# Eight steps of lag in attention, tails without row-wide POOL work, and rows weighed as their gathers land

## The chip, the cores and the metric

The kernel runs on one core of a Trainium2 chip. The metric is the device time of one execution in microseconds (us); lower is better. Engines are called PE (matrix products, with PEld for its weight loads), DVE (vector), ACT (activations), POOL (GpSimd) and SP (the queue that issues most DMAs). Each engine runs its own instructions strictly in the order in which the program emitted them.

## The reference

Input: eight batches of 512 rows with 128 features, float32. Six residual sublayers follow each other:

```python
x = x + 0.5 * moe(layernorm(x))        # stage 0: 8 experts, each row goes to its best 2
x = x + attention(layernorm(x))        # stage 1: 16 heads of 8, causal, rotary positions
x = x + 0.5 * moe(layernorm(x))        # stage 2: the same experts again
x = x + 0.5 * fp6_linear(layernorm(x)) # stage 3
x = x + mixer(layernorm(x))            # stage 4
x = x + 0.5 * fp6_linear(layernorm(x)) # stage 5

def moe(x):        # gates: softmax over the two best scores; y = relu(x W1 + b1) W2 + b2
    return sum(gate[e] * expert[e](x) for e in best_two)

def fp6_linear(x): # blocks of 32: scale = max|x| / 7.5, values rounded to a 6-bit grid
    return dequantized(x) @ dequantized(weight).T + bias

def mixer(x):
    xn = rmsnorm(x) * w1
    h  = scan(h = a * h + sigmoid(g) * tanh(v)), a = 0.001 + 0.998 * sigmoid(d)   # g, v, d: products of xn
    x  = x + h
    xn = rmsnorm(x) * w2
    return x + (silu(xn Wg.T) * (xn Wu.T)) Wo.T
```

## The kernel before

All eight batches stay in SBUF as tiles `X[b]` of 128 partitions x 4 x 128: four groups of 128 rows. The program is one long Python function that emits instructions; the order on each engine is what the generators below yield to each other.

**The planner.** `Clock` (L66) logs every instruction that a generator emits between two yields, adds estimated durations (`took`) and keeps, for each engine, the time at which it would be free, and for each generator the time at which its next step is `ready`. `drive` (L141) follows one main generator and lets side generators step at given rates when they are ready; `finish` (L159) always steps the stream that is ready first. No time of the chip enters: the planner only fixes the order. A step that yields `"product"` must be due; another one may come 0.7 planned us early.

**MoE.** The batches of a MoE stage go in two groups (stage 2: batches 0 to 4, then 5 to 7). A router (`moe_front`, in stage 2 `moe_stream`, batch by batch) scores rows, finds the two best experts and scatters the normed rows with POOL's indirect DMAs into a table in DRAM sorted by expert. `moe_tiles` runs tiles of 256 rows: SP loads the expert's weights and the rows, PE turns and multiplies, ACT and DVE apply relu (`hs`), DVE copies (`xt`) and adds the last bias (`yo`), SP stores to `rows_out`. Stage 2 has 27 tiles for its first group and 19 for its second. `moe_combine` gathers each row's two results from `rows_out` with POOL's indirect DMAs into tiles `y` (six buffers) and weighs them into `X[b]` with two DVE operations for each 128 rows (`put`, which runs when more than three gathered tiles wait). `behind` holds a generator back until a condition is true: the gathers of a group start when all its tiles' stores are emitted (`filled`).

**Attention** runs in steps t; one unit is a batch and one of four head groups, three steps long, and two units make a pair. In step t `maxima` computes scores of unit (t + LAG) // 3 on PE (tiles `sa`) and DVE takes their row maxima (`seen`, into `nstat`); `shifted` turns a pair's maxima on PE (`tp_st`) and adds them into the queries (`qa`); `weights` computes the scores again with the maxima taken off (`sb`), ACT takes the exponentials (`pm`), POOL zeroes what is masked; `values` multiplies by V (`av`). `PIECES_A` and `PIECES_C` list which row blocks a step computes: its scores of four strips of PE run side by side. `pre(b)` (projections, rotary) and `post(b)` are side streams inside the loop. Scores and other products share eight PSUM banks. The stage-2 router and tiles run beside attention as side streams.

**Tails.** After a batch's stage-2 rows are weighed, `tail(b)` does `fp6`, `mix`, `fp6` and the output DMA; up to four tails are in flight (`flight`), and `Slots` limit how many are in a given part. `fp6` (L1277): moments on DVE, a power of -0.5 on POOL, normed rows `um` on ACT, then `quantized` (L1227): block maxima and reciprocals on DVE, the product with the reciprocal on POOL, the rounding by four DVE operations, the product with the scale on POOL; then turned on PE, copied by ACT, multiplied by the weight, and added by DVE. POOL also adds half the bias to `X[b]`. `mix` (L1307) norms twice, one after the other (layer norm to `um_m`, then the rms norm to `row_m`, each with its own power on POOL), runs three gate products, tanh on ACT, the scan on DVE, a second norm from DVE's moments, six products with silu, and the last product; POOL adds `um_m` to `X[b]`.

Most instructions carry the line of the recording helper, L185, so profiles of this kernel are read by tile names.

Of the kernel before, what the change touches and what calls it, by code (L numbers as in the profile page):

```python
# [46 lines left out]
LANDING = 5  # L47
AHEAD = 4
# [17 lines left out]
class Clock:  # L66
# [4 lines left out]
    def __init__(self, nc):  # L71
        self.free = dict.fromkeys(("tensor", "vector", "scalar", "gpsimd"), 0.0)
        self.log = []
        self.ready = {}
        self.slack = {}
        self.flowing = set()
        for name in self.free:
            setattr(self, name, _Logged(getattr(nc, name), name, self.log))
# [19 lines left out]
    def account(self, ready, chained=True):  # L98
# [3 lines left out]
        for engine, op, out, args in self.log:  # L102
# [9 lines left out]
            if op == "indirect_dma_start":  # L112
                end += 0.5
# [3 lines left out]
    def step(self, gen, now):  # L117

        self.log.clear()
        hint = next(gen, gen)  # L120
# [38 lines left out]
    def finish(self, *streams, until=None):  # L159
# [3 lines left out]
        while live and not (until and until()):  # L163
            g = min(live, key=lambda g: max(self.ready.get(g, 0.0), now))
            now = max(now, min(self.ready.get(g, 0.0), max(self.free.values())))
# [69 lines left out]
def kernel(  # L235
# [112 lines left out]
    half_bq = cpool.tile([P, P], F32, tag="half_bq", name="half_bq")  # L348
# [5 lines left out]
    nc.sync.dma_start(out=half_bq, in_=bq.partition_broadcast(P))  # L354
# [6 lines left out]
    def clear_for_attention():  # L361
# [11 lines left out]
        ck.gpsimd.tensor_scalar_mul(half_bq, half_bq, 0.5)  # L373
# [121 lines left out]

    def sent(s, g):
# [8 lines left out]
    def need(s, b):  # L505

        while (s, b) not in done:
            if next(backlog[0], backlog) is backlog:
                backlog.pop(0)
            ck.idle(ck.free["tensor"] + 0.5)  # L510

# [155 lines left out]
    def moe_stream(s, g):  # L667
# [81 lines left out]
        for n, b in enumerate(bs):  # L749
# [16 lines left out]
            ms = []  # L766
            for k in range(2):
# [3 lines left out]
                ck.vector.tensor_tensor(is_max, l, m.to_broadcast([P, NT, NE]), ALU.is_equal)  # L771
                ck.vector.tensor_tensor(is_max, is_max, rank, ALU.mult)
# [10 lines left out]
            ck.vector.tensor_tensor(both, oh[:, 0, sl, :], oh[:, 1, sl, :], ALU.add)  # L783
            ck.vector.tensor_tensor(ex[:, sl].unsqueeze(2), ms[1], ms[0], ALU.subtract)
            yield "product"
# [14 lines left out]
            ck.vector.tensor_tensor(place, place, in_tile, ALU.add)  # L800
            ck.vector.tensor_tensor(
# [6 lines left out]
            )  # L808
            ck.vector.tensor_reduce(at_f[:, :, sl], q, AX.X, ALU.add)
# [22 lines left out]
    def moe_tiles(s):  # L832
# [55 lines left out]
        def second(i, h):  # L888
# [21 lines left out]
            ))  # L910
            del T[i]
# [33 lines left out]
    def moe_combine(s, g):  # L945
# [7 lines left out]
        def put():  # L953
            f, y, t, b = waiting.pop(0)
            f(y, t)
            if t == NT - 1:
                done.add((s, b))

        for n, b in enumerate(GROUPS[s][g]):
# [9 lines left out]
            for t in range(NT):  # L969
# [11 lines left out]
                waiting.append((weighted, y, t, b))  # L981
                if len(waiting) > 3:
                    put()
        while waiting:
            yield
            put()


    def attention(bs, s):
# [6 lines left out]
        PIECES_A = [[(1, 0)], [(3, 0)], [(2, 0), (0, 3 * P)]]  # L996
        PIECES_C = [[(0, 0)], [(1, 0), (3, 3 * P)], [(2, 0)]]
        LAG = 7
# [228 lines left out]
    def quantized(src, g, name, slots=None, also=None):  # L1227
# [19 lines left out]
        ck.gpsimd.tensor_tensor(y, src, along(rs), ALU.mult)  # L1247
        if also:
            also()
        yield  # L1250
# [6 lines left out]
        ck.vector.tensor_scalar(m, m, 1.5, 2.0**20, ALU.max, ALU.mult)  # L1257

        ck.vector.scalar_tensor_tensor(t, y, -(2.0**-21), m, ALU.add, ALU.add)
        ck.vector.tensor_tensor(t, t, m, ALU.subtract)  # L1260
        yield
        ck.gpsimd.tensor_tensor(y, t, along(sc), ALU.mult)
# [14 lines left out]
    def fp6(b, s):  # L1277
# [6 lines left out]
        def plus_bias():  # L1284
            ck.gpsimd.tensor_tensor(
                X[b], X[b], half_bq.unsqueeze(1).to_broadcast([P, NT, P]), ALU.add
            )

        xd = yield from quantized(
            u.rearrange("p t (g k) -> p (t g) k", k=FB), S // FB, name, rounding, plus_bias  # L1290
        )
        yield from turning.take()
        xt = yield from by_feature(xd.rearrange("p (t g) k -> p t (g k)", t=NT), f"xd_{name}")
        rounding.give()
        yp = bank(f"yp_{name}")
        for t in range(NT):
            ck.tensor.matmul(yp[:, ts(t, P)], xt[:, ts(t, P)], wd_t, start=True, stop=True)
# [9 lines left out]
    def mix(b):  # L1307
        mv = moments(X[b], f"m_{b}")
        rs = yield from power(mv[:, :, 1], 1e-5, f"m_{b}")

        r2 = small.tile([P, NT], F32, tag="r2", name=f"r2_{b}")
# [209 lines left out]
```

## Time and profile before

| what | value |
|---|---|
| median of 4 runs | 1194.34 us (1193.94 to 1198.65) |
| the profiled execution | 1199.84 us, its span 1198.1 us |
| mean granted PE clock | 0.901 of full |
| attention's first scores to its last (`sa` to `sb`) | 276.6 to 820.6 us |
| last attention output added | 840.1 us |
| second group's expert tiles (`xp`) | 880.3 to 967.9 us |
| gathers of stage 2, group 0 and group 1 | 876.6 to 981.5, 998.0 to 1065.4 us |
| output stores issued | 1017.2, 1053.5, 1093.6, 1101.1, 1135.6, 1169.0, 1183.2, 1194.8 us |

How to read the profile lines: times count from the first instruction. A group or timeline line has engine, operation, `out<-in` by the program's tile names, partitions x elements, then count, duration (busy us and mean ns in groups) and the idle time of the engine just before, with what ended it. Two operations of one engine may overlap by some tenths of a microsecond. A line of waits is: engine and tile that waited, for whom, us in total, times, longest. A line of a stretch is: stretch, length, busy us (and instructions) of PE, PEld, DVE, ACT, POOL, granted PE clock, DMA share, GB/s. The slices of the page cut the span in 40; each digit is the busy share in tenths.

### The profile page before, as it was taken

The numbers are of one execution on the slowest core, as the hardware profiler recorded it, in microseconds if no ns is written. First come the engines' busy times: TensorE is split into PE (matmuls) and PEld (weight loads), VectorE is DVE, ScalarE is ACT, GpSimd is POOL, SyncE is SP. The second block draws the span as 40 slices with busy tenths as digits, with TensorE's granted clock in tenths as the row PEclk, the third lists the DMA queues.
The fourth block names the chain that finished last, engine by engine and source line by source line (L and its number), as shares of the span: only waits on it lengthen the run. The fifth ranks groups of instructions, "written<-read, shape, count | busy, mean of one in ns | idle before, by whom it ended". The sixth has DMA issues, their size and how long they took to land.

```text
span 1198.1 us, 20686 instructions
## 1 busy us (share of the span) xinstructions
PE 970.6 (81%) x6705; PEld 663.0 (55%) x6705; DVE 706.3 (59%) x2636; ACT 482.8 (40%) x1063; POOL 543.6 (45%) x694
## 2 busy tenths in 40 slices
PE   3261599899999899999999899999969895576583
PEld 2250599787754444444445366667859773344352
DVE  6040132455578877777768765632526867987774
ACT  1210133233255545454555444454314553444351
POOL 3637302511166676536364514132244757765432
PEclk9996799899999998889899999999979997797586
DMA  9542377687386000000000244234467510000000
GB/s 292 178 143 79 124 224 229 205 272 230 114 243 176 21 30 19 19 1 19 1 19 6 81 137 133 87 122 145 127 195 238 167 38 30 24 27 19 9 1 26
DMA packets 122363, 127.33 MB, mean 106 GB/s; under 512 B 9616, under 2 KB 103696, under 8 KB 122256
## 3 DMA queue, kind: packets, MB, share of 16 engines
q1 hardware_dynamic: 114064, 109.22, 29.6%
q0 software_dynamic: 8192, 16.79, 4.4%
q8 instruction: 53, 0.87, 0.3%
q14 instruction: 54, 0.44, 0.1%
HBM read 79.58 MB, written 46.40 MB: 105 GB/s over the span
## 4 chain that ended last, share of the span: by engine, by line
PE 61%; DVE 18%; another core or an unknown queue 6%; issue 5%; POOL 5%; ACT 3%; DMA 1%; SPq 1%; POOLq 0%; DVEq 0%; ACTq 0%
PE yp L185 14%; PE hp L185 13%; PE sa L185 10%; PE av L185 6%; PE sb L185 4%; DVE q L185 3%; DVE seen L185 2%; DVE x L185 2%; POOL y L185 2%; DVE st L185 2%; PE xp L185 2%; PE gt L185 1%; PE lp L185 1%; PE up L185 1%
## 5 line engine op out<-in xcount | busy, mean ns | idle before, releaser
L185 DVE CUSTOM_DVE_ANT_0 seen<-sa,future_s 128x128 f32<-128x128 f32 (+3 forms) x512 | 224.8, 487 | 91.2 <-PE sb L185 69.0
L185 ACT ACTIVATE pm<-sb 128x512 f32<-128x512 f32 (+1 forms) x384 | 182.8, 525 | 191.0 <-PE sb L185 165.2
L185 ACT ACTIVATE hs<-hp,wx 128x256 f32<-128x256 f32 x276 | 120.0, 471 | 313.5 <-PE hp L185 226.7
L185 PE MATMUL yp<-wx,hs 128*128 128x128 f32 x1472 | 204.0, 282 | 46.6 <-ACT hs L185 26.6
L185 PE MATMUL sb<-qa,ka 32*128 32x512 f32 (+3 forms) x1024 | 229.5, 490 | 8.2 <-DVE nstat L185 6.8
L185 PEld LDWEIGHTS yp<-wx,hs 128*128 128x128 f32 x1472 | 189.1, 195 | 63.4 <-ACT hs L185 27.7
L185 PE MATMUL hp<-xt,wx 128*128 128x256 f32 x736 | 200.8, 398 | 8.0 <-DVE g L185 5.3
L185 PE MATMUL sa<-ka,qz 32*128 32x256 f32 (+3 forms) x1024 | 205.5, 485 | 1.6 <-issue 1.6
L185 POOL TENSOR_SCALAR_AFFINE_SELECT pm<-pm 128x256 f32<-128x256 f32 x256 | 101.1, 409 | 215.1 <-ACT pm L185 206.8
L185 POOL DMA_INDIRECT y<-rows_out,at x128 | 134.4, 1050 | 135.9 <-DMA rows_out<-yo 85.7
L185 DVE TENSOR_SCALAR hs<-hp,wx 128x256 f32<-128x256 f32 x92 | 44.5, 483 | 204.2 <-ACT hs L185 178.3
L185 PEld LDWEIGHTS hp<-xt,wx 128*128 128x128 f32 x736 | 133.7, 201 | 31.2 <-issue 10.6
L185 PEld LDWEIGHTS sa<-ka,qz 32*128 32x128 f32 x1024 | 98.1, 192 | 65.9 <-issue 21.4
L185 PEld LDWEIGHTS sb<-qa,ka 32*128 32x128 f32 x1024 | 107.9, 192 | 26.6 <-DVE nstat L185 12.9
L185 PE MATMUL av<-pm,vpad 128*32 128x512 f32 (+3 forms) x1024 | 94.3, 464 | 0.0
L185 POOL DMA_INDIRECT by_stretch<-um,sat x64 | 64.3, 1005 | 30.2 <-issue 14.4
L185 POOL TENSOR_TENSOR rs<-rs,mhalf 128x4 f32<-128x4 f32 (+1 forms) x36 | 39.9, 1109 | 81.6 <-DVE rs L185 77.3
L185 PEld LDWEIGHTS av<-pm,vpad 128*32 128x32 f32 x1024 | 23.7, 110 | 69.4 <-issue 43.2
L185 POOL DMA_INDIRECT rows_in<-a,at x40 | 38.9, 973 | 31.8 <-issue 31.2
L185 DVE TENSOR_TENSOR yo<-yp,wx 128x256 f32<-128x256 f32 x92 | 38.4, 418 | 25.1 <-PE yp L185 10.2
L185 DVE SCALAR_TENSOR_TENSOR x<-y,g,x 128x128 f32<-128x128 f32 x128 | 51.8, 406 | 2.3
L185 PE MATMUL xp<-cst,xs 128*128 128x128 f32 x184 | 37.5, 290 | 16.5 <-DMA xs<-by_stretch 16.5
(219 smaller groups left out, 1316.4 us busy)
## 6 DMA issues: line engine op xcount, KB each, us to landing
wx<-in_wexp SPq DMA_DIRECT2D x92, 578.0 KB
rows_out<-yo SPq DMA_DIRECT2D x92, 128.0 KB
by_stretch<-zero SPq DMA_DIRECT2D x8, 1280.0 KB
rows_in<-zero SPq DMA_DIRECT2D x2, 3456.0 KB
by_stretch<-zero SPq DMA_DIRECT2D x8, 768.0 KB
xs<-rows_in SPq DMA_DIRECT2D x46, 128.0 KB
xs<-by_stretch SPq DMA_DIRECT2D x46, 128.0 KB
x<-in_x SPq DMA_DIRECT2D x8, 256.0 KB
```

What stands on the lines that cost most here:

```text
L185: return call(*args, **kw)
```

## The change

Five things change together.

1. Attention: `LAG` 7 becomes 8, and the first two entries of `PIECES_A` change places. The maxima run one step further ahead of the weights; the same widths lie beside each other as before. What hangs on the lag (`pre`, `masked`, `keyed`) moves one step with it.
2. `fp6`: the two row-wide products of `quantized` move from POOL to DVE. The bias goes into the product's PSUM bank as a matmul of a row of ones with the bias row (K = 1), ahead of the four weight products; POOL's addition and the halving of the bias are gone.
3. `mix`: both scalings of the first two norms come from one power of eight columns; the rms norm's rows `xn` are made first, the layer norm's `u` after the gates. The gate d's affine step moves from DVE to ACT. The second norm's mean square comes from four ACT squares with an accumulated sum instead of DVE's moments. `X[b] + u` is a matmul with the identity into the last product's bank instead of a POOL addition.
4. `moe_combine`: a gathered tile is weighed when the planner's clock is `FETCH` (3 us) past its gather, or when more than four wait; `landed` lets a group's gathers start 5 planned us after its last store instead of at once.
5. The planner: a gather's step is over when issued, other POOL operations cost 0.5 us more, `finish` may move its clock past all engines, and the stage-2 router yields more often (five more in a batch).

```diff
+FETCH = 3
@@ Clock.account
             if op == "indirect_dma_start":
+                end = at
+            elif engine == "gpsimd":
                 end += 0.5
@@ Clock.finish
-            now = max(now, min(self.ready.get(g, 0.0), max(self.free.values())))
+            now = max(now, self.ready.get(g, 0.0))
@@
+    def landed(s, g):
+        return filled(s, g) and ck.now >= groups[s, g]["since"] + LANDING
@@ moe_stream (one of the five places)
                 ck.vector.tensor_tensor(is_max, l, m.to_broadcast([P, NT, NE]), ALU.is_equal)
+                yield
                 ck.vector.tensor_tensor(is_max, is_max, rank, ALU.mult)
...
             ck.vector.tensor_tensor(ex[:, sl].unsqueeze(2), ms[1], ms[0], ALU.subtract)
-            yield "product"
+            yield
@@ moe_combine
+        def come():
+            return ck.now >= waiting[0][-1] + FETCH
...
-                waiting.append((weighted, y, t, b))
-                if len(waiting) > 3:
+                waiting.append((weighted, y, t, b, ck.free["gpsimd"]))
+                while len(waiting) > 4 or (waiting and come()):
                     put()
+                    yield
         while waiting:
-            yield
-            put()
+            if come():
+                put()
+            yield
@@ attention
-        PIECES_A = [[(1, 0)], [(3, 0)], [(2, 0), (0, 3 * P)]]
+        PIECES_A = [[(3, 0)], [(1, 0)], [(2, 0), (0, 3 * P)]]
...
-        LAG = 7
+        LAG = 8
@@ quantized
-        ck.gpsimd.tensor_tensor(y, src, along(rs), ALU.mult)
-        if also:
-            also()
-        yield
+        ck.vector.tensor_tensor(y, src, along(rs), ALU.mult)
...
         ck.vector.tensor_tensor(t, t, m, ALU.subtract)
-        yield
-        ck.gpsimd.tensor_tensor(y, t, along(sc), ALU.mult)
+        ck.vector.tensor_tensor(y, t, along(sc), ALU.mult)
@@ fp6
-        def plus_bias():
-            ck.gpsimd.tensor_tensor(
-                X[b], X[b], half_bq.unsqueeze(1).to_broadcast([P, NT, P]), ALU.add
-            )
...
+        ck.tensor.matmul(
+            yp.rearrange("p (t d) -> p t d", t=NT), ones[0:1, :],
+            bq_s[0:1].unsqueeze(1).to_broadcast([1, NT, P]), start=True, stop=False,
+        )
@@ mix
-        rs = yield from power(mv[:, :, 1], 1e-5, f"m_{b}")
-        r2 = small.tile([P, NT], F32, tag="r2", name=f"r2_{b}")
-        ck.vector.tensor_tensor(r2, rs, rs, ALU.mult)
-        ck.vector.tensor_tensor(r2, r2, mv[:, :, 1], ALU.mult)
-        u = yield from normed_act(X[b], mv, rs, f"m_{b}", tag="um")
-        rr = yield from power(r2, 1e-6, f"ma_{b}")
-        ck.vector.tensor_tensor(rr, rr, rs, ALU.mult)
-        xn = yield from normed_act(X[b], mv, rr, f"m_{b}", tag="row")
+        ck.vector.tensor_scalar(
+            rs2[:, 1], mv[:, :, 1], 1.0 + 1e-6, 1e-6 * 1e-5, ALU.mult, ALU.add
+        )
+        ck.vector.tensor_scalar_add(rs2[:, 0], mv[:, :, 1], 1e-5)
+        yield
+        ck.gpsimd.tensor_tensor(
+            rs2, rs2, mhalf[:, 0 : 2 * NT].rearrange("p (k t) -> p k t", k=2), ALU.pow
+        )
...
+        scaled(xn, 1, 0, NT)
...
-        ck.vector.tensor_scalar(d, d, 0.499, 0.5, ALU.mult, ALU.add)
+        ck.scalar.activation(d, d, AF.Copy, scale=0.499, bias=0.5)
+        scaled(u, 0, 0, NT)
...
-        mv = moments(u, f"f_{b}")
+            ck.scalar.activation(
+                xf[:, t, :], u[:, t, :], AF.Square, accum_out=r2[:, t : t + 1]
+            )
...
-        ck.gpsimd.tensor_tensor(X[b], X[b], u, ALU.add)
...
         yo = bank(f"yo_{b}")
+        ck.tensor.matmul(yo, ident, uf, start=True, stop=False)
@@
-    back = behind(moe_combine(2, 0), lambda: filled(2, 0) and sent(2, 1))
+    back = behind(moe_combine(2, 0), lambda: landed(2, 0) and sent(2, 1))
...
-    last = behind(moe_combine(2, 1), lambda: filled(2, 1))
+    last = behind(moe_combine(2, 1), lambda: landed(2, 1))
```

## The prediction

> **What bounds the kernel now.** I read the page first (busy shares and the slices), then the busy times by stretch, then the chain of waits and the waits of single engines in the stretches that the change touches, and last the timeline of the final fp6 pass.
>
> ```profile
> PE 970.6 (81%) x6705; PEld 663.0 (55%) x6705; DVE 706.3 (59%) x2636; ACT 482.8 (40%) x1063; POOL 543.6 (45%) x694
> ...
> PE   3261599899999899999999899999969895576583
> ...
> DVE  6040132455578877777768765632526867987774
> ...
> POOL 3637302511166676536364514132244757765432
> ```
> ```profile
> 275.00:845.00 570.00, 539.28 (x4339) 313.72 (x4340) 376.65 (x1569) 274.82 (x596) 255.77 (x412) 0.95 0.28 84
> 845.00:880.00 35.00, 26.17 (x171) 23.56 (x169) 15.89 (x65) 8.43 (x21) 10.61 (x11) 0.92 0.36 111
> 880.00:1000.00 120.00, 98.77 (x598) 84.57 (x598) 80.80 (x258) 50.41 (x113) 66.58 (x63) 0.90 0.49 151
> 1000.00:1125.00 125.00, 78.02 (x320) 50.42 (x320) 103.68 (x306) 55.24 (x124) 82.78 (x77) 0.73 0.07 21
> 1125.00:1198.00 73.00, 48.93 (x201) 31.50 (x200) 41.52 (x118) 28.60 (x61) 22.78 (x20) 0.76 0.04 15
> ```
> Each row gives the stretch, its length, then PE, PEld, DVE, ACT and POOL busy, the granted clock, DMA. Attention (275 to 845) is PE's: 539 of 570 us. From 880 to 1000 the last expert tiles run beside the first tails, PE still ahead with 99 of 120. From 1000 on it is tails alone: DVE has 104 of 125 us and POOL 83, PE 78 at a clock of 0.73. After 1125 no engine is near full; the last batches wait through their own chains. From 905, just before the first tail's start at 911, to the end DVE is busy 219.5 of 293 us.
>
> The chain of waits between 1000 and 1125, summed by engine from its pieces, is DVE 71 us, POOL 26, issue 16, PE 6, ACT 5: two engines hand rows to and fro. The final fp6 pass shows how:
>
> ```profile
> 1183.93 0.25 DVE L185 RECIPROCAL rs<-sc 128x16 f32<-128x16 f32 x1
> 1184.35 1.05 POOL L185 TENSOR_TENSOR q<-um,rs 128x512 f32<-128x512 f32 x1 [4.07 <-DVE rs L185]
> 1185.36 1.26 POOL L185 TENSOR_TENSOR x<-x,half_bq 128x512 f32<-128x512 f32 x1
> 1185.44 1.93 DVE L185 TENSOR_SCALAR q<-q 128x512 int32<-128x512 int32 x2 [1.25 <-POOL q L185]
> 1187.40 0.69 DVE L185 SCALAR_TENSOR_TENSOR q<-q,q 128x512 f32<-128x512 f32 x1
> 1188.13 0.69 DVE L185 TENSOR_TENSOR q<-q,q 128x512 f32<-128x512 f32 x1
> 1188.96 1.05 POOL L185 TENSOR_TENSOR q<-q,sc 128x512 f32<-128x512 f32 x1 [2.34 <-DVE q L185]
> ```
> PE's transposes start at 1190.06. Two things cost: POOL takes 1.05 us where DVE's like form takes 0.69, with a handover each way; and the two TENSOR_SCALARs take 1.93 beside POOL's bias add, where the pair takes 0.88 with POOL silent (1154.87). Taking each DVE form's undisturbed duration off its instructions from 905 to 1198, 30 us are excess, 29 of them overlapping POOL's row-wide operations (bias 12.4, x<-x,um_m 7.4, q 9.5) and 0.6 its gathers; 18 us of it lie between 1000 and 1125.
>
> Waits, as engine, whom it waited for, us, times, longest: of POOL (880 to 1070), DVE (1000 to 1125), PE (275 to 850).
> ```profile
> POOL y L185 <- DVE x L185: 9.6, 2, 7.7
> ...
> POOL y L185 <- DMA rows_out<-yo: 6.2, 1, 6.2
> ```
> ```profile
> DVE q L185 <- POOL q L185: 7.7, 2, 6.4
> ```
> ```profile
> PE tp_st L185 <- DVE nstat L185: 7.2, 5, 2.1
> PE sb L185 <- DVE nstat L185: 6.8, 10, 1.5
> ...
> PE pt L185 <- DVE k L185: 3.7, 2, 2.4
> PE pt L185 <- DVE ex L185: 2.7, 3, 0.9
> ```
>
> **The change part by part.** The profiled execution took 1199.84 us (span 1198.1), 5.5 over the median of the runs; I take savings from its trace and subtract them from 1194.3.
>
> *Attention.* With LAG 8 the last maxima of a pair end one step (57 us a batch / 12 = 4.8) before their transposes, which wait at most 2.1: the 7.2 of tp_st goes. Widths beside each other stay as they are, since the order of PIECES_A is turned with the lag. What is late next is a PSUM bank held by DVE (the sb row): of its 6.8 I take 2. The projection vp holds its bank one step longer and all five ka buffers are now in use; no wait on either is in the trace, so 0 to 4.8 a batch, nearer nothing: +2. The finer router steps put pt behind its operands in PE's order: half of 6.4. Together -10 (bounds -18 to +20). The router gets five more yields a batch at two per half step of 2.4 us, so its scatters end 6 us later; attention alone leaves PE 8% idle, so that costs 0.5, and a little on the last batch, whose scatter is exposed (845 to 880): +1 (0 to +6).
>
> *Rows weighed as they come.* The first gather lands near 879, but its rows are weighed at 898.65, behind tile operations in DVE's queue; POOL stands 7.7 us for a y buffer, and the first tail starts at 911. DVE is half idle there. With three planned us instead of three further tiles, the tail could start up to 18 us earlier; I take 8 (0 to 18), since that moment is the planner's, not the chip's. `landed` keeps the second gather from standing on POOL (6.2), behind which the q of two batches queued (DVE idle 6.4): -5 (0 to -6.4). Queued behind that gather now is nothing; a gather released too late would cost the last three batches alone.
>
> *fp6, twice a batch.* Removed from POOL: two q operations of 1.05 and the bias of 1.27, 16 times, 54 us. Added to DVE: two of 0.69, 16 times, 22 us. Added to PE: one 1x512 product; nearest row, a 128x512 one (gt, two instructions), 0.86 to 2.07 us by the clock of the moment. From reciprocal to transposes 5.9 us become 3.9 (four at 0.69, the pair at 0.88, gaps).
>
> *mix, once a batch.* Of three POOL powers two become one, a POOL add (1.45) becomes a 512-wide PE product, and one 1.65 us run of scalings leaves the path to the gates. DVE loses the second moments (4 x 0.28 + 4 x 0.15 less overlap, 1.25), two r2f operations (0.32), gtd (0.42) and five small ones at 0.16: 2.8 us, 22 for eight batches, the same as fp6 adds. So DVE's work stays, and its excess goes. ACT gains four squares (Copy with a pointer scale: 0.39; Identity: 0.48) and gtd (0.58): 2.4 a batch, 20 us on an engine 44% busy between 1000 and 1125; the cover is that slack, and without it up to 2.4 a batch shows. The tile um_m is now read until PE's yo, 17 us longer (its POOL reader starts at 1156.1, the yo it would wait for at 1173.2); four tails in flight hold one each of four buffers, so that costs nothing, and up to 17 us where a fifth is wanted. The output stores on SP's queue wait for the same last DVE addition as before, and no DMA is added.
>
> *Sum of the tails.* Between 1000 and 1125: the 18 us of excess, and of POOL's 26 on the chain about a third, 9, because gathers and powers stay and PE and ACT come next: -27 (-12 to -40). After 1125: two passes at -2.0, and the shorter start of mix, some -2: -6 (-3 to -12). The 24 new PE products are 21 us warm; in the 10 that fall before 1000 PE is half of the chain, later it is mostly covered: +6 (+2 to +25).
>
> -10 + 1 - 8 - 5 - 27 - 6 + 6 = -49: 1145 us (1151 for a profiled execution).
>
> *A rule against the trace.* After 840 the trace of before has a single load of ACT's tables, of 1.28 us, although tanh and silu alternate there with copies and identities; it has no square. If every run of squares needed a switch there and back, 16 loads of 1.28 would put 20 us on ACT; the bounds are 0 and 20, and I take 0, since none of the functions that stand beside it causes one. The Trainium skill (ScalarE: Activation LUTs, What ACT_TABLE_LOAD costs) speaks against the change here: it gives 2.66 us with its drain for each switch to another set of functions, and by it the 16 would make 43 us and the sum only -6. No run here shows that drain.
>
> **The rivals.**
> A, denser: with POOL out of the way DVE runs from first tail to last store at the 83% it has between 1000 and 1125. 190 us of DVE (219.5 less 29) make 229 instead of 293; with the earlier start and attention, 64 + 8 + 9 = 81 less: 1113. For it: the work is there. Against: the last 73 us are one chain.
> B, little: the freed link is taken by PE and ACT at a clock of 0.73, and the planner's clock misses the chip's, so that "as they come" and `landed` do nothing. Two thirds of the excess (12), 4 at the end, 3 in attention, 3 given back to PE: 16 less, 1178.
> C, slower: DVE's queue becomes the tiles' gate. From 887 to 970 nineteen tiles need three DVE operations each, in order behind whatever tails were emitted first; fp6 now puts runs of 1.6 and 2.1 us there (before, one of 2.3). It decides from 49 / 19 = 2.6 us a tile; both runs before each tile, 3.6, make 69 lost: 1214. Against: PE waited for hs 2.8 us in all in that stage, and no run gets longer.
>
> **How the numbers follow.** The forecast 0.55, A 0.12, B 0.18, C 0.12, and 0.03 for a change lost in what can be told from none, 0.3% or 3.6 us. Faster are the forecast, A and B: 0.85. The forecast's own range is 1125 to 1167; taking in B and most of A gives 1110 to 1188 and leaves out C and the edge of A.
>
> **What would show it.** Right: no tp_st wait on nstat, DVE's TENSOR_SCALAR q near 0.43 after 905 (0.75 now), POOL under 110 us there (160), first tail before 905, reciprocal to transposes 4 us. Wrong: ACT table loads in the tails, hs waits on DVE of over 2 us a tile, PE over 90% busy after 1000, or PE idle in attention above the present 31 us.

## The result, and the profile after

| | median us | runs |
|---|---|---|
| before | 1194.99 | 55 (1189.34 to 1207.28) |
| after | 1196.70 | 34 (1183.71 to 1205.38) |

The ratio is 1.000, 95% interval 0.9986 to 1.0014: no difference, where 1145 us had been forecast. The profiled execution of after took 1206.33 us (span 1204.6), a slow one, 9.6 above its median; two more profiles of the same kernel (e5 and e17 below, spans 1193.6 and 1193.3) stand beside it wherever a difference is small.

The page of after, the same four rows as before: busy shares, then the slices.

```profile
PE 999.7 (83%) x6753; PEld 695.9 (58%) x6753; DVE 683.3 (57%) x2550; ACT 494.3 (41%) x1135; POOL 472.9 (39%) x627
...
PE   3251599799998998999898999999967888987695
...
DVE  6030133455566788867677756541524675689755
...
POOL 3637302330136658646353514223115452165210
```

POOL lost 71 us of work, DVE 23; PE gained 29. The stretches (PE, PEld, DVE, ACT, POOL busy, clock, DMA):

```profile
275.00:845.00 570.00, 536.16 (x4313) 336.82 (x4312) 371.87 (x1535) 271.53 (x588) 250.93 (x408) 0.95 0.27 83
845.00:880.00 35.00, 31.74 (x217) 28.51 (x216) 17.18 (x73) 12.44 (x30) 8.88 (x9) 1.00 0.42 132
880.00:1000.00 120.00, 95.58 (x497) 76.41 (x498) 65.83 (x211) 46.84 (x119) 49.34 (x46) 0.87 0.50 154
1000.00:1125.00 125.00, 104.52 (x472) 68.14 (x470) 92.20 (x277) 64.77 (x163) 48.67 (x43) 0.88 0.09 29
1125.00:1205.00 80.00, 55.33 (x228) 32.97 (x228) 46.19 (x119) 34.58 (x93) 9.05 (x8) 0.83 0.04 14
```

From 1000 to 1125 PE has 104.5 of 125 us where it had 78, at a granted clock of 0.88 where it had 0.73 (99 and 100 us at 0.90 and 0.89 in e5 and e17). The chain of waits there, summed by engine, was DVE 71, POOL 26, issue 16, PE 6, ACT 5; it is now PE 55, DVE 47, ACT 15, issue 6, POOL 2. In e5 and e17 DVE is ahead of PE, 56 to 43 and 53 to 46, with ACT at 17. Two engines handed rows to and fro; now three do, and PE holds nearly as much of the chain as DVE, or more.

The final fp6 pass, in the timeline, is what the prediction made of it:

```profile
1191.27 0.25 DVE L190 RECIPROCAL rs<-sc 128x16 f32<-128x16 f32 x1
1191.56 0.69 DVE L190 TENSOR_TENSOR q<-um,rs 128x512 f32<-128x512 f32 x1
1192.28 0.89 DVE L190 TENSOR_SCALAR q<-q 128x512 int32<-128x512 int32 x2
...
1194.66 0.69 DVE L190 TENSOR_TENSOR q<-q,sc 128x512 f32<-128x512 f32 x1
1195.40 0.71 PEld L190 LDWEIGHTS tp_xd<-cst,q 128*128 128x128 f32 x4 [7.47 <-DVE q L190]
```

From the end of the reciprocal to the transposes it takes 3.9 us (5.9 before); the pair of TENSOR_SCALARs takes 0.89 (1.93 beside POOL's bias).

So the tails' local steps came true and the total did not move. Four stretches, cut at the first and last attention output, the first gather of stage 2 and the last output store, show where it went:

| us | first attention output | to the last one | to the first gather | to the last store | last store |
|---|---|---|---|---|---|
| before | 397.3 | 442.8 | 36.5 | 318.2 | 1194.8 |
| after | 404.4 | 446.3 | 51.3 | 299.3 | 1201.3 |
| after again (e5) | 407.6 | 441.5 | 49.0 | 292.2 | 1190.3 |
| after again (e17) | 401.9 | 445.9 | 51.2 | 290.9 | 1189.9 |

The stretch that the tails fill is 19 to 27 us shorter. Attention is as long as before, the first gather comes 12 to 15 us later after it, and attention's first output itself is 5 to 10 us late. In the profiles these two eat all but some 5 us of the gain.

**The first gather.** SP's queue and POOL's first gather before:

```profile
852.87 21.49 SPq L908 DMA_DIRECT2D rows_out<-yo  x6
875.21 0.36 SPq L843 DMA_DIRECT2D wx<-in_wexp  x1
```
```profile
876.60 1.07 POOL L185 DMA_INDIRECT y<-rows_out,at  x1 [11.31 <-DMA rows_out<-yo]
```

SP's queue and DVE's last group-0 output, from the timeline of after, then POOL:

```profile
864.85 19.61 SPq L922 DMA_DIRECT2D rows_out<-yo  x5
885.32 0.36 SPq L857 DMA_DIRECT2D wx<-in_wexp  x1
887.08 0.39 SPq L868 DMA_DIRECT2D xs<-by_stretch  x1
...
896.40 0.37 SPq L868 DMA_DIRECT2D xs<-by_stretch  x1
896.87 0.41 SPq L922 DMA_DIRECT2D rows_out<-yo  x1
```
```profile
885.72 0.42 DVE L190 TENSOR_TENSOR yo<-yp,wx 128x256 f32<-128x256 f32 x1 [1.65 <-PE yp L190]
```
```profile
876.30 0.97 POOL L190 DMA_INDIRECT by_stretch<-um,sat  x1 [0.30 <-issue]
902.01 1.07 POOL L190 DMA_INDIRECT y<-rows_out,at  x1 [24.74 <-DMA xs<-by_stretch]
```

The last rows of group 0 are ready at 886.1. Their store is issued at 896.87, behind five pairs of loads for group 1 that stand ahead of it on SP's queue, 2.3 us a pair. Only then can the first gather start, at 902; POOL stood 24.7 us. (The profile names a load as releaser here; in e5's the same wait is put down to the store.) Before, all six stores went ahead of the loads and the gather came at 876.6, 2.6 us after the last of them was issued.

**The lag.** The waits of PE from 275 to 850, as engine, whom it waited for, us, times, longest:

```profile
PE pt L190 <- DVE k L190: 9.4, 4, 2.6
PE tp_st L190 <- DVE nstat L190: 6.9, 5, 1.6
PE sb L190 <- DVE nstat L190: 4.8, 5, 1.7
```

The wait of tp_st was to vanish. It is 6.9 us, 5 times (7.0 in e5 and e17); it was 7.2, 5 times. Counting DVE's maxima (32 for a pair) shows that the cause has changed. Before, the 32nd of a pair ended 0.05 to 0.18 us before the pair's transposes in 14 of 16 pairs: PE waited for its data. After, it ended 4.0 to 12.8 us before them (median 6.15) in every pair. What ends the wait is a maximum of the *next* pair, as here:

```profile
522.83 0.36 DVE L190 BATCH_NORM_AGGREGATE mv<-st 128x2 f32<-128x6 f32 x4
523.23 0.17 DVE L190 TENSOR_SCALAR rs<-mv 128x4 f32<-128x4 f32 x1
523.32 0.68 DVE L190 CUSTOM_DVE_ANT_0 seen<-sa,future_s 128x512 f32<-128x512 f32 x1
523.92 0.08 DVE L190 DVE_READ_ACCUMULATOR2_ANT nstat<- 128x1 f32 x1
...
524.06 0.66 PE L190 MATMUL tp_st<-cst,nstat 128*128 128x128 f32 x4 [1.42 <-DVE nstat L190]
```

The statistics of attention's finished rows hold DVE, the row maximum of the next scores comes after them, and the transposes start when it has ended. The reason is the bank. The scores and the transposes share the eight PSUM banks, and the built program says which tile had a bank before and what each instruction waits for. In all five pairs that wait, the transposes take over the bank of the third score tile of the next pair, and their wait on DVE is for the maximum read from that tile; in the trace just three maxima of the next pair have ended when they start. In the program of before, the wait of its five waiting pairs is for the pair's own last maximum.

### The profile page after: what moved, and what is told of

The parts are those of the page before. It is cut to its first block, busy times and chain, and to the rows that moved or that the text cites. A ratio compares the mean times of both kernels' runs of the same rounds, so it can differ in the third digit from the quotient of the medians.

```text
span 1204.6 us, 20637 instructions
## 1 busy us (share of the span) xinstructions
PE 999.7 (83%) x6753; PEld 695.9 (58%) x6753; DVE 683.3 (57%) x2550; ACT 494.3 (41%) x1135; POOL 472.9 (39%) x627
## 4 chain that ended last, share of the span: by engine, by line
PE 61%; DVE 17%; another core or an unknown queue 7%; issue 5%; ACT 4%; POOL 3%; DMA 2%; SPq 1%; POOLq 0%; ACTq 0%; DVEq 0%
PE yp L190 15%; PE hp L190 13%; PE sa L190 9%; PE av L190 6%; PE sb L190 5%; DVE q L190 3%; DVE seen L190 2%; DVE x L190 2%; DVE st L190 2%; PE xp L190 1%; PE gt L190 1%; ACT um L190 1%; PE yo L190 1%; PE up L190 1%
## 5 line engine op out<-in xcount | busy, mean ns | idle before, releaser
L190 PE MATMUL yp<-wx,hs 128*128 128x128 f32 x1472 | 207.7, 284 | 50.1 <-issue 25.4
L190 PEld LDWEIGHTS yp<-wx,hs 128*128 128x128 f32 x1472 | 193.2, 198 | 70.1 <-issue 36.7
L190 PE MATMUL sb<-qa,ka 32*128 32x512 f32 (+3 forms) x1024 | 224.9, 491 | 6.7 <-DVE nstat L190 4.8
L190 PE MATMUL sa<-ka,qz 32*128 32x512 f32 (+3 forms) x1024 | 213.6, 489 | 3.6 <-DVE nstat L190 2.5
L190 PEld LDWEIGHTS sa<-ka,qz 32*128 32x128 f32 x1024 | 108.0, 196 | 72.9 <-issue 24.1
L190 PEld LDWEIGHTS sb<-qa,ka 32*128 32x128 f32 x1024 | 104.6, 191 | 30.6 <-DVE nstat L190 7.2
L190 POOL TENSOR_TENSOR rs<-rs,mhalf 128x4 f32<-128x4 f32 (+2 forms) x44 | 53.4, 1213 | 169.1 <-DVE rs L190 139.7
L190 PE MATMUL av<-pm,vpad 128*32 128x512 f32 (+3 forms) x1024 | 97.5, 478 | 2.9 <-POOL pm L190 2.7
L190 DVE SCALAR_TENSOR_TENSOR x<-y,g,x 128x128 f32<-128x128 f32 x128 | 46.7, 369 | 12.5 <-DMA y<-rows_out,at 6.0
L190 DVE COPY xt<-xp 128x256 f32<-128x256 f32 x92 | 38.0, 415 | 15.3 <-PE xp L190 12.0
```

What stands on the lines that cost most here:

```text
L190: return call(*args, **kw)
```

## The experiments

Five features were put in or left out: *tails* (fp6, quantized, mix), *combine* (weighing by the planner's clock, `landed`), *planner* (prices of POOL, `finish`), *yields* (stage-2 router) and *lag* (LAG 8 with PIECES_A). The whole change has all five.

The chips were of two kinds. On some (the first comparison, e5 to e12, e17, e18) before takes 1190 to 1196 us; on others (e1 to e4, e13 to e16) 1125, since the last tile of stage 0 begins (its `xp`) near 255 us instead of 318. Ratios are each against before on the same chip; times and profiles are compared within one kind only.

**e1, the tails alone, in the kernel before.**
```diff
-        ck.gpsimd.tensor_tensor(y, src, along(rs), ALU.mult)
+        ck.vector.tensor_tensor(y, src, along(rs), ALU.mult)
...
```
The diffs of `quantized`, `fp6` and `mix` as in the change, and nothing else of it.


> The kernel before with the new fp6 and mix alone; planner, combine, router and attention as before. Theory O (the order of emission took the gain: the second group's expert tiles end 49 us later in the changed kernel, and the last three batches with them): the old planner keeps those tiles ending near 970 us, and the time falls by 25 to 45 us, to 1150 to 1170. Rival P (PE became the bound of the tails, through 24 new 512-wide products): the time stays within 8 us of 1194, PE above 80% busy from 1000 on.


1127.17 us, ratio 1.0034 (1.0013 to 1.0054). The tails alone gain nothing, although the second group's tiles end early here (their last `yo` at 931.0; 951.2 in e4, which is faster), so theory O falls: a late end of these tiles is not what took the gain here. From 835 to 1125 DVE's excess over undisturbed durations beside POOL's operations is 0.5 us (30.3 in e3, whose tails are the old ones), so that part of the argument holds. But PE is busy 228.5 us where e3 has 199.1, and of the chain PE has 127 (e3: 85), DVE 80 (108), POOL 18 (36).

**e2, all but the tails.**
```diff
-        ck.vector.tensor_tensor(y, src, along(rs), ALU.mult)
+        ck.gpsimd.tensor_tensor(y, src, along(rs), ALU.mult)
...
```
The tails are those of before; lag, combine, planner and yields those of after.


> The changed kernel with the old fp6 and mix (row-wide POOL work, no new PE products). Theory O: the tiles of the second group end late here too (after 1000 us), POOL's row-wide work is back, and the time is 1205 to 1225. Rival P: with PE's new products gone the other parts show their gain, 1175 to 1188.


1155.59 us, ratio 1.0239 (1.0181 to 1.0298). With the old tails the other four cost 2.4%, about what theory O said of the time. DVE's excess is 37.9 us here, and DVE has 119 us of the chain from 835 to 1125.

**e3, the lag alone, in the kernel before.**
```diff
-        PIECES_A = [[(1, 0)], [(3, 0)], [(2, 0), (0, 3 * P)]]
+        PIECES_A = [[(3, 0)], [(1, 0)], [(2, 0), (0, 3 * P)]]
-        LAG = 7
+        LAG = 8
```


> The kernel before with LAG 8 and the turned PIECES_A alone. The changed kernel adds its last attention output 10.6 us later than before (850.7 to 840.1). If the lag does that: last attention output near 850, time 1200 to 1206. If the lag is innocent (the router's yields or the planner do it): output at 835 to 842, time 1186 to 1196. Either way the waits of tp_st on nstat should be gone, if the lag does what it is for.


1126.07 us, ratio 1.0024 (0.9998 to 1.0051). No gain; the predicted 10 us would be 0.991. The wait of tp_st on nstat, which was to be gone here, is 7.1 us, 5 times, in the stretch of attention (210 to 780; 5.9 us, 5 times, in e1).

**e4, tails, combine and planner, without lag and yields.**
```diff
-        LAG = 8
+        LAG = 7
...
```
PIECES_A and the router's yields are those of before too.


> The changed kernel with LAG 7 and the old router yields. If lag and yields cost the 10 us at 850, the time is 1184 to 1190, all of it gained before 850; if the planner's new costs do it, the last attention output stays near 850 and the time at 1193 to 1200. Theory O: the second group's tiles still end after 1000 us.


1105.14 us, ratio 0.9835 (0.98 to 0.9869): faster by 1.65%, 2% below e1, although its first gather is 14 us later than e1's (817.9 to 803.5). From first gather to last store it takes 278 us, e1 316. So combine and planner together turn the faster tails into time; which part of them does it is seen in e14.

The next four ran on a chip where before takes 1192.84.

**e5, the whole change again,** without an edit.


> The whole change beside its partial forms, on the chip of e1 to e4 if it is the same one. Theory M (what the tails and the combine win, the attention part and the finer router steps give back): 1.00 of the kernel before, as measured first, about 20 us above e4; the last attention output at 780 to 790 us in place of e4's 771.6. Theory N (the first comparison's chip had a late start that hid a gain): 0.98 to 0.985, like e4.


1196.03 us, ratio 1.0023 (1.0004 to 1.0042). The result stands. Its stretches are in the table above.

**e6, without the router's yields.**
```diff
-                yield
...
-            yield
+            yield "product"
```
Five yields of `moe_stream` go, and one is a "product" again.


> The whole change but for the stage-2 router's additional yields. If the finer router steps are what gives e4's gain back (theory M, router): near e4, 0.98 to 0.985 of before. If the lag does (theory M, lag): 0.995 to 1.005. If only the two together disturb the order: 0.98 to 0.99, and e7 likewise.


1204.05 us, ratio 1.0082 (1.0054 to 1.0111). The yields do not cost; without them it is slower, which none of the three expectations had. Its last three stores come 42, 53 and 64 us after the fifth, in e5 33, 41 and 54: a different order at the end.

**e7, without the lag.**
```diff
-        PIECES_A = [[(3, 0)], [(1, 0)], [(2, 0), (0, 3 * P)]]
+        PIECES_A = [[(1, 0)], [(3, 0)], [(2, 0), (0, 3 * P)]]
-        LAG = 8
+        LAG = 7
```


> The whole change but with LAG 7 and the old order of the first two pieces. If the lag gives e4's gain back: 0.98 to 0.985. If the router's yields do: 0.995 to 1.005. If each gives back a part: 0.987 to 0.995 here and in e6.


1184.46 us, ratio 0.9915 (0.9869 to 0.9961). In the range named for "each gives back a part", but e6 is not, and the reason is not attention: from first to last attention output e7 takes 440.7 us, e5 441.5. Its first attention output is 5 us earlier (402.2 and 407.6), and its first gather 20: POOL waits 7.9 us for it here, 22.4 in e5. The first gather in the timelines of POOL, e7 and then e5:

```profile
878.21 1.07 POOL L190 DMA_INDIRECT y<-rows_out,at  x1 [7.90 <-DMA rows_out<-yo]
```
```profile
898.07 1.07 POOL L190 DMA_INDIRECT y<-rows_out,at  x1 [22.37 <-DMA rows_out<-yo]
```

Here the sixth store of group 0 went ahead of the loads, as in before. The lag changed an order elsewhere. It is not the only part that does: five pairs of loads stand ahead of that store in e2, e3, e4, e6, e10, e11, e13 and every profile of after, none in before, e1, e7, e8, e14 and e15, so the lag alone (e3) brings them there, and so do tails, combine and planner without it (e4, e10).

**e8, the tails alone, less PE's 24 products.** The output lacks the fp6 bias and the addition of u in mix.
```diff
-        ck.tensor.matmul(
-            yp.rearrange("p (t d) -> p t d", t=NT), ones[0:1, :],
-            bq_s[0:1].unsqueeze(1).to_broadcast([1, NT, P]), start=True, stop=False,
-        )
...
-        ck.tensor.matmul(yo, ident, uf, start=True, stop=False)
```


> As e1 (the new fp6 and mix alone), with the 24 new PE products left out: the fp6 bias is not added, and in mix the row X + u lacks u. Theory P (PE took the chain from DVE and POOL, the products being most of what it gained): 15 to 25 us below e1, 0.98 to 0.99 of before, PE's share of the chain after 835 from 127 back to about 105 us. Rival R (the rest of the new order, not these products, holds the end): within 5 us of e1, 1.00 of before.


1181.05 us, ratio 0.9879 (0.9843 to 0.9915). That is what theory P said, but the tails with the products had run on the other kind of chip only, so it is a hint and e11 the test. Its first attention output comes at 393.4, before's at 397.3, though stage 0 and attention are alike in both: single profiles on chips of one kind differ by that much.

**e9, the whole change with group 0's stores first.** Same chip as e5 (before 1190.18 in this comparison).
```diff
-            while loaded < min(i + AHEAD + 1, n) and sent(s, order[loaded][0]):
+            while (
+                loaded < min(i + AHEAD + 1, n) and sent(s, order[loaded][0])
+                and (s == 0 or order[loaded][0] == 0 or filled(s, 0))
+            ):
```


> The whole change, with one condition more in the loading of expert tiles: stage 2's group 1 is loaded only when the last store of group 0 has been emitted, so that this store stands ahead of the loads on SP's queue. Theory Q (with the lag, the last store of group 0 went behind five loads on SP's queue; the first gather waits for it, 22.4 us in e5 where it is 7.9 in e7): first gather 12 to 15 us earlier than e5's 898, the whole 10 to 14 us faster than e5, 0.987 to 0.993 of before, as e7. Rival G (the end hangs on group 1's tiles and gathers, which do not start earlier by it): the first gather is earlier all the same, but the time stays at 0.998 to 1.005.


1190.03 us, ratio 0.9992 (0.9968 to 1.0016). The mechanism is shown: all six stores go ahead of the loads and the first gather comes at 883.9, 14 us before e5's.

```profile
856.94 0.37 SPq L868 DMA_DIRECT2D xs<-by_stretch  x1
859.09 22.57 SPq L922 DMA_DIRECT2D rows_out<-yo  x6
884.29 0.39 SPq L868 DMA_DIRECT2D xs<-by_stretch  x1
```
```profile
883.90 1.07 POOL L190 DMA_INDIRECT y<-rows_out,at  x1 [12.38 <-DMA rows_out<-yo]
```

Its worth was overrated: the last store comes 7 us earlier than e5's in the profiles, the medians differ by 0.3% (about 4 us), and the two intervals overlap. From first gather to last store e9 takes 299.1 us, e5 292.2; the rest of the gain is lost on the way, as rival G said of all of it. It is lost at once: the first rows are weighed at 901.3 in e9 and 901.2 in e5, and the first tail's moments start at 909.7 and 916.8, 7 us apart as the last stores are. In both, the last store comes 91.7 us after the last gather of group 1 (1091.3 and 1098.6).

**e10, e4's kernel on this chip.** The edit is e4's.


> e4's kernel (tails, combine, planner, but neither the lag nor the finer router steps) beside e5 to e9. Theory Q: there is no lag here, so the gain of e4 comes with the order of the queue: 0.983 to 0.992 if on this chip too few loads stand ahead of the last store. Rival H (e4's gain was that of a chip whose first tiles end 60 us earlier): 0.995 to 1.003 on a chip where before takes about 1193 us.


1189.67 us, ratio 0.999 (0.997 to 1.001). Theory H: what gains 1.65% on one kind of chip gains nothing on the other. The loads stand ahead of the store here too (first gather 898.3, 51 us after the last attention output) as they did in e4 (46 us), so the queue does not explain the difference between the chips. From first gather to last store e10 takes 289.6 us and e4 278.3; PE is busy 240 us of it at a granted clock of 0.89 here, 230 us at 0.93 in e4. Why the clock differs is not known.

**e11, the whole change with the bias in one bf16 pass.**
```diff
-            yp.rearrange("p (t d) -> p t d", t=NT), ones[0:1, :],
-            bq_s[0:1].unsqueeze(1).to_broadcast([1, NT, P]), start=True, stop=False,
+            yp.rearrange("p (t d) -> p t d", t=NT), ones_h[0:3, :],
+            bq_h[0:3].unsqueeze(1).to_broadcast([3, NT, P]), start=True, stop=False,
```
Row k of `bq_h` holds the k-th bf16 part of the bias, made once in stage 0; `ones_h` holds bf16 ones.


> The whole change, with the fp6 bias row split once into three bf16 parts on three partitions, so that the 16 products of the bias are one bf16 pass each (3x512) in place of two float32 instructions of 0.82 us (1x512, 23.6 us in e5 after 880). Theory P (PE holds the chain after 1000, and the products are part of that): 16 us less of PE busy, 8 to 14 us faster than e5, 0.988 to 0.995. Rival R (the order, not PE's work, holds the end): within 4 us of e5, 0.998 to 1.004.


1190.60 us, ratio 1.0011 (0.9985 to 1.0036). Groups of PE after 880 in after, then in e11 (operands, count, busy us, mean ns):

```profile
L190 PE MATMUL yp<-bq_s,ones 1*128 1x512 f32 x32 | 23.6, 826 | 0.0
L190 PE MATMUL yo<-um_m,cst 128*128 128x512 f32 x16 | 8.2, 593 | 0.0
```
```profile
L190 PE MATMUL yp<-bq_s 3*128 3x512 bf16 x16 | 7.0, 439 | 0.0
```

The products' time falls from 23.6 to 7.0 us, and the whole is within 0.2% of e5. So the length of the bias products is not what holds the end of the whole change, against theory P: rival R. The eight products of `X[b] + u` were left as they are. In the profile the tails' stretch is 7 us shorter than e5's (285.1), but attention and the stretch to the first gather take 7 us more, and the last store comes 3.7 us earlier (1186.6).

**e12, e4's kernel with e9's and e11's edits.**


> Tails, combine and planner of the change without lag and finer router steps, with e9's condition and e11's bias. If theories Q and P both hold: 0.965 to 0.98 of before, 1150 to 1169 us where before takes 1193. If only one does: 0.98 to 0.99.


1178.20 us, ratio 0.9896 (0.9854 to 0.9938), faster than both kernels by 1%. That is the range for only one of the two theories. Against e10, on the same chip, its first gather is 14 us earlier and its last store 14.4.

The next four ran on a chip where before takes 1124.83.

**e13, the whole change with the old weighing rule in stage 0.**
```diff
+                if s == 0:
+                    if len(waiting) > 3:
+                        put()
+                    continue
                 while len(waiting) > 4 or (waiting and come()):
...
+            if s == 0:
+                yield
+                put()
+                continue
```


> The whole change, but the combine of stage 0 keeps the old rule (weigh when more than three gathered tiles wait); stage 2 keeps the new one. Theory U (weighing as the planner's clock says puts DVE behind gathers in stage 0, whose tiles then end 12 to 16 us later, and the first attention output 6 to 10 us later): tiles of stage 0 end at 316 to 322 us in place of 332 to 334, the first attention output at 396 to 400 in place of 404 to 408, the whole 0.99 to 0.995 of before. Rival V (the planner's new prices of POOL's operations did that): the tiles still end at 330 to 335, 0.998 to 1.005.


1114.10 us, ratio 0.9918 (0.9899 to 0.9937). The whole change had not run on this kind of chip, so this says little before e18: the last tile of stage 0 begins at 262.3 us, e4's with the new rule at 264.0.

**e14, the whole change with the old prices of POOL.**
```diff
             if op == "indirect_dma_start":
-                end = at
-            elif engine == "gpsimd":
                 end += 0.5
```


> The whole change, but the planner counts POOL's operations as before (0.5 us more only after a gather). Theory U: the tiles of stage 0 still end at 330 to 335 us and the first attention output at 402 to 408; 0.998 to 1.005 of before. Rival V: 316 to 322 and 396 to 400 us, 0.99 to 0.995.


1127.49 us, ratio 1.0033 (1.0011 to 1.0055). First attention output 340.1 us, later than e13's 335.6: the new prices are not what delays it. The first gather comes 35.5 us after the last attention output, and still the end is later: from first gather to last store 314 us, e13 280.5. Part of that is only the earlier gather (804.8 and 827.4), but the last store is 11 us later too (1118.9 and 1107.9) and the median 13. The other difference from e13, the rule in stage 0, is worth 0.3% in e17 and e18. So with the new weighing rule and the old prices of POOL the gain is gone, as in e1: the rule alone is not what turns the faster tails into time.

**e15, the tails alone again.** The edit is e1's.


> e1's kernel (the new fp6 and mix alone) on the chip of e5 to e12, if it is that one. Theory P (PE's products take back what POOL and DVE lose): 1.00 to 1.007 of before, some 15 us above e8, which leaves the products out. Rival R (e8's gain is of the tails as such): 0.985 to 0.992, near e8.


1128.11 us, ratio 1.0018 (0.9997 to 1.0038). As e1.

**e16, e12 with e13's edit.**


> e12 (tails, combine and planner without lag and finer router steps, group 0's last stores ahead of group 1's loads, bias in one bf16 pass), with the old rule in stage 0's combine. Theory U: 6 to 10 us below e12, 0.980 to 0.985 of before. Rival V: as e12, 0.988 to 0.992.


1103.19 us, ratio 0.9805 (0.9781 to 0.983): the fastest ratio seen and in theory U's range, though its interval meets e4's. Its first attention output is at 332.4 us, e1's at 333.0.

**e17 and e18, the whole change and e13's kernel, on one chip** (before 1196.43).


> The whole change once more, beside e18. If this is the chip of e1 to e4 and e13 to e16 (before takes about 1125 us there), the whole change has not run on it: theory S (as on the other chip) 1.00, theory H (its gain depends on the chip) 0.99 to 0.995. If it is the other chip: 0.998 to 1.004, as e5.


1200.57 us, ratio 1.0028 (1.001 to 1.0046).


> e13's kernel beside the whole change. Theory U: 0.4 to 0.8% below e17, the first attention output 4 to 8 us before e17's. Rival V (the new rule in stage 0 costs nothing, e13's 0.992 is that of the chip): within 0.2% of e17, the first attention output within 2 us of e17's.


1195.37 us, ratio 0.9998 (0.9973 to 1.0022), 0.3% below e17. The last tile of stage 0 begins at 326.9 us (e17 331.6, before 318.0), but the first attention output is at 402.1 and 401.9. Theory U falls in what it said of that output; the small gain lies later, within attention (438.8 to 445.9), and is of the size by which profiles of one kernel differ (441.5 and 445.9 for the whole change).

## Why the prediction was wrong

The forecast was 49 us of gain and none came. Four of its steps failed: the wait of tp_st did not go, the queue of the first gather was not looked at, busy time taken from the tails was counted as span, and stage 0 was put at nothing.

*Attention, −10 (7.2 of it tp_st).* Wrong. The maxima do come a step earlier, 6.15 us in the median where it was 0.15, in every kernel with the lag, and the wait stays. The step that failed is "the 7.2 of tp_st goes": a PSUM bank was seen as what is late next, but only for the sb row, and the transposes wait for one too (7.2 us before, 6.9 after). From first to last attention output five kernels without the lag on the slower kind of chip (before, e7, e8, e10, e12) take 440.7 to 445.5 us, mean 442.8; seven with it 438.8 to 446.3, mean 443.6. On the faster kind e1, e4, e15 and e16 without it and e2, e3, e13 and e14 with it have the same mean, 439.7. PE's idle time in attention is 33.8 us (30.7 before), one of the signs named for wrong, and the wait of pt was not halved but went from 6.4 to 9.4.

*Router, +1.* The order of e6 shows no cost of the yields.

*Rows weighed as they come, −8, and the gather wait, −5.* Counted from the first gather the −8 holds: the first tail's moments start 34.2 us after it before, 25.8 in e9 and 25.6 in e7, where all stores go ahead of the loads. But the gather itself is late. In after the rows are weighed 4 us after it, and still the first tail starts at 920.8 us, 910.8 before. The step that failed is that the start of the gathers was taken from the trace of before: POOL waits 24.7 us ahead of the first one and 4.8 ahead of the second group's (6.2 before). The working looked at what `landed` takes from POOL's queue and not at what stands ahead of the stores on SP's. e9 shows this cause, and also that undoing it is worth some 4 us at the end and not 14.

*Tails, −27, and the end, −6.* The sub-steps hold: excess gone, POOL 104.7 us after 905 (under 110 was forecast), TENSOR_SCALAR 0.44 each, 3.9 us from reciprocal to transposes. Two readings slipped without harm to the sum: the pair at 1154.87 ran beside a power of four columns on POOL (1155.04), not beside a silent POOL, and the first product into yo starts at 1170.4, so um_m is held 14 us longer and not 17. ACT's 20 us cost nothing that shows, and the eight runs of squares no table load: one load after 800 us in both traces (965.8 before, 989.0 after), ahead of the first silu. The Trainium skill (ScalarE: Activation LUTs, What ACT_TABLE_LOAD costs), weighed against the change, gives 2.66 us for a switch with its drain. The traces differ, and they decide: this one switch leaves 1.32 us between ACT's operations before and 1.31 after, which is the load of 1.28 us and no drain.

The step that failed is the passage from busy time to span. From first gather to last store the forecast's terms make −40 (−8, −5, −27, −6, +6); 19 to 27 came, and 19 where the gather is in time (e7 and e9). Of the chain between 1000 and 1125 DVE and POOL lost 48 us and issue 10, and PE took 49 and ACT 10 (in e5 and e17: 38 and 41 lost, 37 and 40 taken by PE, 11 by ACT). Rival B had said that PE and ACT take the freed link, at a lower clock (0.73). The 24 products took 32 us after 880 instead of 21, but e11 shows that the length of the bias products is not what decides in the whole change. Whether all 24 hold the end of the tails alone (e8) stays open.

*What sets the end now.* The last three batches' tails follow their rows alone, so the end hangs on those rows, and the rows come later: the last of them leaves the expert tiles (`yo`) at 1053.8 us and not 995.2, and their gathers start 2.6 us after that. The tiles share PE and DVE with the tails of the first five batches:

| us | first `xp` to last `yo` of the second group | PE busy with tails in it | last gather to last store |
|---|---|---|---|
| before | 115 | 23 | 129 |
| after | 164 | 58 | 91 |
| e5, e17 (after again) | 155, 154 | 55, 55 | 92, 92 |
| e3 (faster kind; lag alone) | 114 | 24 | 130 |
| e1 (faster kind; tails alone) | 124 | 35 | 131 |
| e2 (faster kind; all but the tails) | 127 | 27 | 131 |
| e14 (faster kind; whole, old prices of POOL) | 132 | 44 | 113 |
| e4 (faster kind; no lag, no yields) | 146 | 54 | 90 |

The tails alone stretch the tiles by 10 us, the new order with the old tails by 13; both together do it by 32 (e4 against e3) to 49 (after against before). PE then does 30 to 35 us more of the tails' work before the last tile has ended, and less is left after the last gather: on the slower chips this is work moved, not time saved. The rival C of the prediction named this place, through DVE. PE's waits for hs there are 5.6 us on ACT and 1.5 on DVE (3.6 and 1.0 in e5), so it is not DVE's queue alone.

*Left out altogether:* the combine and the planner's prices run in stage 0 too, and the first attention output is 5 to 10 us late, although attention's first scores come 10 to 13 us earlier (264 to 266 us; 276.6 before). Neither e14 nor e18 brings it back, each undoing one of the two. On the faster chips lag and rule seem to share the delay: 333.0 us in e1, 337.9 with the lag alone (e3), 335.1 with the rule and no lag (e4), 332.4 with neither (e16). On the slower chips the output is late without the lag too (402.2 in e7), and lag and rule were not undone together there; the cause stays open, as does why the same kernel (e4, e10) gains 1.65% on one kind of chip and nothing on the other.

## What to carry to other kernels

Where order is written by a planner, list for each edit the queues that it re-orders, the DMA queue of loads and stores first: a store that someone waits for can land behind loads that nobody needs yet. Before an operand is made earlier, see what else the waiting instruction needs (a bank, a buffer), since the wait may keep its length and change its cause. Work taken from two engines of a chain need not shorten the span by as much, since a third can take up the chain (here PE); check it with a cut at the last arrival of data (here the last gather, after which 91 us follow where it was 129), and look at when that data arrives.

## What the runs showed of the hardware

- A 1x512 float32 product (one row of ones) is no cheaper than a 128x512 one: 826 ns an instruction, two of them, against 593. The same bias as a 3x512 bf16 product takes 439 ns, once.
- The clock granted to PE was higher where PE had more work: from 1000 to 1125 us it was 0.73 with 78 of 125 us busy (before), 0.88 with 104.5 (after), 0.90 with 99 (e5).
- The one switch of ACT's tables in the tails cost its load of 1.28 us and no more: ACT's operations on both sides of it stand 1.32 us apart.
- Chips differ by 6% in this kernel (1125 and 1190 to 1196 us), nearly all of it before attention: first expert rows on PE at 60 and 68 to 72 us, the last tile of stage 0 begun at 255 and 318 for kernels with before's order there. Ratios do not carry from one kind to the other (0.9835 and 0.999 for one kernel).
